# Edge sums by quarters of a group, a packed list in 96 partitions, and edge distances made on chip in a graph layer

## The chip, the cores and the metric

The kernel runs on one core of a Trainium2 chip. The metric is the device time of one execution in microseconds (us), as the median of several runs. TensorE is called PE (its weight loads PEld), VectorE DVE, ScalarE ACT, GpSimd POOL and SyncE SP. Line numbers such as L235 are those of the kernel before the change.

## The reference

`x` holds 6250 nodes of 64 features. 206250 edges are sorted by their target `dst`; each has a source `src` and 64 features of its own.

```python
h = jnp.maximum(_layernorm(x, axis=-1), 0.0)
msg = h[src] + edge_attr_64
agg = jax.ops.segment_sum(msg, dst, num_segments=6250)
y = jax.nn.relu(agg @ W1 + b1) @ W2 + b2
return x + y
```

## The kernel before

**Groups.** The edges are cut into G = 202 groups of 1024 (128 partitions by J = 8 edges). Of these, the first GA = 176 are the main groups and the last GP = 26 the part groups. The sum over `edge_attr_64` is made for all groups in the same way, by `sum_groups` (L227), two groups (GB = 2) at a time. As the edges are sorted, the targets of a group lie close together. DVE makes a mask `hot` (L229): for each edge a row of W = 40 numbers, one where the distance of the edge's target from the group's first target (`rel`) equals the column, else zero. PE multiplies, for each of the eight edges of a partition, the 128 edges' 64 features (as weights) by the mask (as moving operand, 40 columns) and sums in PSUM, `pa` (L235); even and odd edges go to the two halves of the partitions. The line appears twice in the profile's count for each product, since a product in f32 is two matmul instructions. One call later DVE adds `pa` to `agg` at the group's base (`add_sums`, L224); the base is a number in a register that DVE's sequencer reads (`read_bases`, four groups at a time in the main groups, L241).

`load` (L214) brings the features of two main groups by one DMA from SP's queue, three calls ahead; each partition receives its eight edges as one piece of 2 KB per group.

**The sum over h[src].** For the main groups it is made by counting. Every 84 windows of three nodes form one of NW = 22 batches, and a batch has 14 steps. At a step (`count`, L455) DVE makes the masks `hot_lo` and `hot_key` from the lists of sources (`keys`), PE multiplies them into a table of counts (L467) and ACT copies it out (L469). In the batch after, PE multiplies the counts by h, held as three bf16 pieces (`multiply`, L484 and L487), into `pv`, which DVE adds to `agg` (L499). For the part groups POOL gathers the rows of h instead and adds them to the edges' features by DMA (`fetch_h`, 208 gathers, L184).

**The lists.** The prologue makes them. `dst_g` is loaded as `dstn` (row q holds two groups of 1024 targets), `src` is transposed on PE into the same order (L270, copied out by ACT, L271), and DVE joins both into one word per edge (L277). The first QA = 89 rows are stored to DRAM as `packed` (L280, ACT's queue, 712 KB). For each of 1920 windows POOL then gathers 129 words from `packed` (`fetch_words`), from the place of the window's first edge. That place is found by gathers of rows of `dst_g` (`fetch_row`) and counts by DVE (`find`, L199 to L204). `unpack` (L322) splits the words on DVE (L326 to L331), transposes them on PE (L335, L336) and copies them to `keys` on ACT (L339).

`rel` is made by one DVE subtraction (L285) from `dst`, a load of all targets in the order of the groups (L111, 808 KB), less `row2`, the first targets of the groups, which a PE product (`pe`, L273) spreads to all partitions.

**The order.** All instructions of an engine run in the order in which the program writes them (`manual_schedule`). The step loop (L624) goes over 308 steps; before a step it runs what the table `before` (L591) holds for it: layer norm and lists up to step 11, `limits` at step 12, `seconds` at step 13 (the lists of windows with more edges than one gather takes) and the start of the part groups' gathers. From step 14 on, `features` (main groups) and `features_h` (part groups) are spread evenly over the steps. `limits` (L443) is one ACT pass over `rel`, which sums in `bad` what lies beyond the width of the mask, and one DVE comparison that does not read it. After the loop come the last batch's products and node blocks, and one DVE, PE and DVE sequence which decides whether the data fitted the shapes; if not, a slower loop computes all again, which the present data never enter.

**The nodes' network.** `mlp_hidden`, `mlp_product`, `mlp_add`, `mlp_store` (L534 to L555) run on blocks of up to 252 nodes as these become complete.

Of the kernel before, what the change touches and what calls it, by code (L numbers as in the profile page):

```python
# [18 lines left out]
P = 128  # L19
N = 6250  # L20
E = 206250
D = 64
# [8 lines left out]
J = 8  # L31
# [1 line left out]
GN = 256  # L33
GB = 2

W = 40
WR = 128
WR_BITS = 7
ACOLS = N + W + WR


GP = 26
# [37 lines left out]
def gnn_kernel(ctx: ExitStack, tc: tile.TileContext, x, src_t, dst_t, dst_g, edge, w1, b1, w2, b2, out):  # L80
# [47 lines left out]
    nc.scalar.activation(agg, zero.to_broadcast([P, ACOLS]), AF.Copy)  # L128

    HW = V * P  # L130
    iota_hw = small.tile([P, IC + 1], F32, name="iota_hw")
# [72 lines left out]
        nc.vector.tensor_scalar(first_i[:, i0:i0 + n], to, float(EA), None, op0=OP.min)  # L204


    rel = dst.bitcast(F32)
    base_i = consts.tile([1, G], I32, name="base_i")
    feats = {}
    bases = {}  # L210
# [3 lines left out]
    def load(g):  # L214
        feats[g] = work.tile([P, GB * J, D], F32, name="feat", bufs=3)
        nc.sync.dma_start(
            feats[g].rearrange("p (b j) d -> p b (j d)", j=J),
            edge[g * P * J:(g + GB) * P * J, :].rearrange("(b p j) d -> p b (j d)", p=P, j=J))

    def add_sums():  # L220
        for g, pa in to_add:
            for b in range(GB):
                to = agg[:, ds(bases.pop(g + b), W)]
                nc.vector.tensor_tensor(to, to, pa[:, b, :], op=OP.add)  # L224
        to_add.clear()

    def sum_groups(g, tiles):  # L227
        hot = work.tile([P, GB, J, W], F32, name="hot")
        nc.vector.tensor_tensor(hot, rel[:, g:g + GB, :].unsqueeze(3).to_broadcast([P, GB, J, W]),  # L229
                                iota[:, :W].unsqueeze(1).unsqueeze(1).to_broadcast([P, GB, J, W]), op=OP.is_equal)  # L230
        pa = ps.tile([P, GB, W], F32, tag="pa", name="pa")
        for b in range(GB):
            for j in range(J):
                k = j % 2 * D
                nc.tensor.matmul(pa[k:k + D, b, :], tiles[b][:, j, :], hot[:, b, j, :], start=(j < 2),  # L235
                                 stop=(j >= J - 2))
            done_at[g + b] = made[0] if g < GA else max(made)
        add_sums()
        to_add.append((g, pa))
# [24 lines left out]
    srcf = src.bitcast(F32)  # L264
    nc.scalar.activation(srcf, src, AF.Copy)
    srcv = srcf.rearrange("p (q h j) -> p q h j", h=2, j=J)
    for h in range(2):
        pt = ps.tile([P, J, P], F32, tag="pc", name="psrc")
        for j in range(J):
            nc.tensor.transpose(pt[:GA // 2, j, :], srcv[:, :, h, j], ident)  # L270
        nc.scalar.activation(srcl[:GA // 2, h].rearrange("q p j -> q j p"), pt[:GA // 2], AF.Copy)  # L271
# [10 lines left out]
    find(1, 2)  # L282
    for i in range(6, 9):
        fetch_row(i)
    nc.vector.tensor_tensor(rel, dst, row2.unsqueeze(2).to_broadcast([P, G, J]), op=OP.subtract)  # L285
# [144 lines left out]

    bad = small.tile([P, 2], F32, name="bad")
    edge_w = small.tile([P, 1], F32, name="edge_w")
    nc.gpsimd.memset(edge_w, 1.0 - W)
# [5 lines left out]
    evs = small.tile([P, NW * STEPS], F32, name="evs")  # L441

    def limits():  # L443
        nc.scalar.activation(late.tile([P, G * J], BF16, tag="part", name="over", bufs=2), rel.rearrange("p g j -> p (g j)"),
                             AF.Relu, bias=edge_w, accum_out=bad[:, 0:1])
        nc.vector.tensor_tensor(needed, row2[0:1, :], needed, op=OP.is_lt)


# [229 lines left out]
    sums = small.tile([1, 4], F32, name="sums")  # L678
    nc.vector.tensor_reduce(bad[:, 1:2], evs, AX.X, OP.add)
    pb = ps.tile([P, 2], F32, tag="pv", name="pb")  # L680
    nc.tensor.matmul(pb, ones, bad, start=True, stop=True)
    nc.vector.tensor_reduce(sums[:, 2:3], needed, AX.X, OP.max)
    nc.vector.tensor_scalar(sums[:, 0:1], pb[:1, 0:1], 0.0, None, op0=OP.is_gt)
    nc.vector.tensor_scalar(sums[:, 1:2], pb[:1, 1:2], float(EA), None, op0=OP.not_equal)
    odd_i = small.tile([1, 1], I32, name="odd_i")
    nc.vector.tensor_reduce(sums[:, 3:4], sums[:, :3], AX.X, OP.add)
    nc.vector.tensor_copy(odd_i, sums[:, 3:4])
    order.__exit__(None, None, None)


# [1 line left out]
    with tc.If(odd > 0):  # L692
        nc.vector.memset(agg, 0.0)

        dst2 = counts[0].rearrange("p h n -> p (h n)").bitcast(I32)[:, :2 * P * J].rearrange("p (h k) -> p h k", h=2)
        nc.sync.dma_start(dst2, dst_g)
        top = small.tile([P, 2], F32, name="top")
        nc.vector.tensor_reduce(top, dst2, AX.X, OP.max)
        diag2 = work.tile([P, P, 2], F32, tag="hot", name="diag2")
        nc.vector.tensor_tensor(diag2, ident.unsqueeze(2).to_broadcast([P, P, 2]),  # L700
                                top.unsqueeze(1).to_broadcast([P, P, 2]), op=OP.mult)
        pe2 = ps.tile([P, GN], F32, tag="pv", name="pe2")
        nc.tensor.matmul(pe2, ones, diag2.rearrange("p q h -> p (q h)"), start=True, stop=True)
        wide = small.tile([1, G], F32, name="wide")
        nc.vector.tensor_tensor(wide, pe2[0:1, :G], row2[0:1, :], op=OP.subtract)
        wide_i = small.tile([1, G], I32, name="wide_i")
        nc.vector.tensor_scalar(wide_i, wide, float(WR), None, op0=OP.add)
        nc.vector.tensor_scalar(wide_i, wide_i, WR_BITS, None, op0=OP.arith_shift_right)
        with tc.For_i(0, G, 1) as g:
            feat = work.tile([P, J, D], F32, tag="pfeat", bufs=4, name="feat2")  # L710
            hsrc = work.tile([P, J, D], F32, tag="pfeat", bufs=4, name="hsrc")
            nc.sync.dma_start(feat.rearrange("p j d -> p (j d)"),
                              edge.rearrange("(g p j) d -> g p (j d)", p=P, j=J)[ds(g, 1), :, :]
                              .rearrange("o p f -> (o p) f"))
            index = work.tile([P, J], I32, name="index", bufs=1)
            nc.sync.dma_start(index, src_t[:, ds(g * J, J)])
            left = work.tile([P, J], F32, name="left", bufs=1)
            nc.vector.tensor_copy(left, rel.rearrange("p g j -> p (g j)")[:, ds(g * J, J)])
# [58 lines left out]
```

## Time and profile before

| | |
|---|---|
| median of 3 runs | 604.29 us (603.38 to 604.59) |
| the profiled execution | 606.77 us, of which the profile's span is 605.1 us |
| mean granted PE clock | 0.905 |
| PE busy | 487.0 us (80% of the span) |
| DVE busy | 491.5 us (81%) |
| POOL busy | 401.7 us (66%) |
| ACT busy | 345.9 us (57%) |
| moved by DMA | 73.96 MB in 75905 packets |

The profile comes from one execution. "Busy" is the time in which an engine had an instruction at work. In lists of groups of instructions, a row has the line, the engine, the operation, the output and inputs with their shapes and the count; then the busy time of all and the mean of one in ns; then the idle time of the engine just before them and what ended it. In a timeline a row has the start, the length and the instruction, and in brackets the wait before it. In a list of waits the numbers are the total in us, the times and the longest. In the view by windows, the window and its length are followed by the busy time of PE, PEld, DVE, ACT and POOL with their instructions, the granted PE clock, the DMA share and GB/s. The queue q1 is SP's, q10 ACT's and q0 POOL's; after a queue's name stand packets, MB and the share of the time of 16 DMA engines.

### The profile page before, as it was taken

What the parts mean: (1) busy time and instruction counts of PE and PEld (TensorE: products, weight loads), DVE (VectorE), ACT (ScalarE), POOL (GpSimd) and SP (SyncE); (2) the same over time, 40 slices, a digit from 0 to 9 for tenths busy, and PEclk for the clock granted to TensorE, in tenths of its full rate; (3) what the DMA queues carried; (4) which work ended last, traced back from release to release, by engine and by line L of the source; (5) the groups of instructions that cost most, each with busy time, mean ns of one, the idle gap of its engine ahead of it and who ended that gap; (6) DMA issues with size and microseconds to landing.
All of it is one profiled execution on the core that took longest, in us unless ns stands there. A gap on an engine that the chain in (4) does not pass through costs nothing.

```text
span 605.1 us, 18376 instructions
## 1 busy us (share of the span) xinstructions
PE 487.0 (80%) x7529; PEld 410.5 (68%) x7530; DVE 491.5 (81%) x1120; ACT 345.9 (57%) x688; POOL 401.7 (66%) x258
## 2 busy tenths in 40 slices
PE   3000234799898998999999999999999999999993
PEld 2000123688786777788887887878888887888872
DVE  5501989699899988899998898898998899899821
ACT  7000467577575655666665665666666666666630
POOL 4503620588888888888888888888888888860000
PEclk9555555599999999999999999999999999999996
DMA  9701244156655654565655555465656565553000
GB/s 255 229 27 53 57 88 111 38 144 143 177 138 130 148 131 120 131 159 129 156 126 148 117 142 145 121 154 129 156 134 156 126 149 119 125 140 113 8 1 17
DMA packets 75905, 73.96 MB, mean 122 GB/s; under 512 B 40709, under 2 KB 48767, under 8 KB 75599
## 3 DMA queue, kind: packets, MB, share of 16 engines
q1 hardware_dynamic: 44398, 61.49, 32.6%
q0 software_dynamic: 31184, 9.80, 14.9%
q8 instruction: 61, 1.00, 0.7%
q10 hardware_dynamic: 234, 1.45, 0.6%
q14 instruction: 28, 0.23, 0.1%
HBM read 68.77 MB, written 3.93 MB: 120 GB/s over the span
## 4 chain that ended last, share of the span: by engine, by line
PE 62%; DVE 18%; issue 10%; ACT 3%; DMA 3%; DVEq 1%; POOL 0%; ACTq 0%
PE pc L467 19%; PE pv L484 15%; PE pa L235 12%; PE pv L487 10%; DVE hot_key L461 6%; DVE hot_lo L461 4%; DMA rows<-in_dst_g,row_i 2%; PE po L545 2%; DVE hot L229 2%; PE ph L538 2%; DVE agg L224 2%; ACT counts L469 1%; ACT keys L339 1%; DMA firsts_i<-in_dst_g 1%; PE pk L335 1%
## 5 line engine op out<-in xcount | busy, mean ns | idle before, releaser
L184 POOL DMA_INDIRECT pfeat<-table,src_p x208 | 365.2, 1756 | 63.4 <-issue 58.8
L469 ACT ACTIVATE counts<-pc 128x882 bf16<-128x882 f32 x308 | 279.8, 910 | 174.4 <-PE pc L467 157.5
L467 PE MATMUL pc<-hot_key,hot_lo 128*128 128x147 bf16 x1848 | 177.3, 234 | 34.8 <-DVE hot_key L461 27.8
L461 DVE TENSOR_TENSOR hot_key<-iota_key,keys 128x888 bf16<-128x888 bf16 x308 | 189.7, 616 | 0.0
L467 PEld LDWEIGHTS <-hot_lo 128*128 128x128 bf16 x1848 | 128.8, 100 | 66.2 <-DVE hot_key L461 39.1
L461 DVE TENSOR_TENSOR hot_lo<-iota_lo,keys 128x768 bf16<-128x768 bf16 x308 | 169.5, 550 | 1.1 <-issue 0.6
L484 PE MATMUL pv<-counts,h 128*128 128x252 bf16 x1078 | 147.5, 270 | 0.4 <-ACT counts L469 0.4
L484 PEld LDWEIGHTS <-h 128*128 128x128 bf16 x1078 | 98.8, 97 | 8.6 <-issue 0.6
L235 PEld LDWEIGHTS pa<-hot,feat 128*64 128x64 f32 x2816 | 92.7, 139 | 14.3 <-DVE hot L229 4.1
L235 PE MATMUL pa<-hot,feat 128*64 128x40 f32 x2816 | 100.2, 230 | 2.4 <-DVE hot L229 2.2
L229 DVE TENSOR_TENSOR hot<-dst,iota 128x640 f32<-128x640 f32 x101 | 82.5, 817 | 3.4 <-issue 3.4
L487 PE MATMUL pv<-counts,h 128*64 128x252 bf16 x1078 | 81.4, 276 | 0.0
L487 PEld LDWEIGHTS <-h 128*64 128x64 bf16 x1078 | 53.3, 109 | 14.8 <-issue 4.6
L469 ACT ACTIVATION_READ_ACCUMULATOR counts<-pc 128x1 f32 x308 | 59.4, 193 | 0.0
L335 PE MATMUL pk<-ident,klo 128*128 128x128 f32 (+1 forms) x16 | 7.0, 436 | 58.5 <-ACT klo L329 58.5
L224 DVE TENSOR_TENSOR agg<-agg,pa 128x40 f32 x202 | 38.9, 193 | 16.6 <-PE ph L538 5.7
L184 POOL DMA_INDIRECT words<-packed,first_i x15 | 15.6, 1042 | 44.6 <-DMA packed<-dstn 27.5
L335 PEld LDWEIGHTS pk<-ident,klo 128*128 128x128 f32 (+1 forms) x16 | 3.2, 200 | 61.3 <-ACT klo L329 61.3
L550 DVE TENSOR_TENSOR y<-xs,po 126x128 f32<-126x128 f32 (+2 forms) x25 | 7.2, 288 | 34.6 <-PE po L545 33.1
L329 ACT ACTIVATE klo<-klo 128x256 f32<-128x256 int32 (+2 forms) x9 | 3.5, 386 | 42.1 <-DVE klo L326 42.1
L184 POOL DMA_INDIRECT rows<-in_dst_g,row_i x15 | 16.6, 1104 | 11.6 <-DVE row_i L181 6.5
L326 DVE TENSOR_SCALAR klo<-words 128x256 int32<-128x256 int32 (+2 forms) x9 | 2.4, 270 | 25.6 <-DMA words<-packed,first_i 25.6
(125 smaller groups left out, 230.2 us busy)
## 6 DMA issues: line engine op xcount, KB each, us to landing
feat<-in_edge SPq DMA_DIRECT2D x88, 512.0 KB
pfeat<-in_edge SPq DMA_DIRECT2D x26, 256.0 KB
pfeat<-table,src_p POOLq DMA_INDIRECT x208
out_y<-y SPq DMA_DIRECT2D x23, 63.0 KB
dstn<-in_dst_g SPq DMA_DIRECT2D x1, 1024.0 KB
table<-xl SPq DMA_DIRECT2D x2, 512.0 KB
xs<-in_x SPq DMA_DIRECT2D x3, 315.0 KB
dst<-in_dst_t SPq DMA_DIRECT2D x1, 808.0 KB
```

The source lines that it names most:

```text
L184: nc.gpsimd.indirect_dma_start(out=rows, out_offset=None, in_=source, in_offset=bass.IndirectOffsetOnAxis(ap=index, axis=0), compute_op=op)
L224: nc.vector.tensor_tensor(to, to, pa[:, b, :], op=OP.add)
L229: nc.vector.tensor_tensor(hot, rel[:, g:g + GB, :].unsqueeze(3).to_broadcast([P, GB, J, W]), iota[:, :W].unsqueeze(1).unsqueeze(1).to_broa ...
L235: nc.tensor.matmul(pa[k:k + D, b, :], tiles[b][:, j, :], hot[:, b, j, :], start=(j < 2), stop=(j >= J - 2))
L335: nc.tensor.transpose(pk[:, 0, i, :p], klof[:p, i, :], ident[:p, :p])
L461: nc.vector.tensor_tensor(hot.rearrange("p t (m o) -> p t m o", o=2), iota_k.rearrange("p (m o) -> p m o", o=2).unsqueeze(1).to_broadcast( ...
L467: nc.tensor.matmul(pc[:, k, m * K:(m + 1) * K], hot_lo[:, j, :], hot_key[:, j, :K], start=True, stop=True)
L469: nc.scalar.activation(counts[b % 2][:, :, s * ST * V:(s + 1) * ST * V].rearrange("p h (k m) -> p h k m", k=2), pc[:, :, :ST // 2 * K].rea ...
L484: nc.tensor.matmul(pv, h3[:, h, :2 * D], counts[b % 2][:, h, :], start=(h == 0), stop=False)
L487: nc.tensor.matmul(pv[k:k + D, :], h3[:, h, 2 * D:], counts[b % 2][:, h, :], start=False, stop=(h >= HI - 2))
L538: nc.tensor.matmul(ph[:, :n], w1s, agg[:, start[b]:start[b + 1]], start=True, stop=True)
L545: nc.tensor.matmul(po[:pairs[b], k, :], outs[b][:, k:2 * pairs[b]:2], w2s, start=True, stop=True)
```

## The change

- **Quarters.** The edges of a main group are laid out in four quarters (JQ = 4) of 256 edges; in a quarter, a partition holds two edges (JP = 2). The mask of an edge is WQ = 18 columns wide, and the window of quarter q starts 8q - 5 nodes from the group's base; the matmul writes 18 of the 42 columns of `pa` (W = 8 x 3 + 18). A load of features has pieces of 512 B in place of 2 KB. The part groups keep whole groups, with W = 42.
- **Room below the base.** `agg` becomes a view of `sums`, which has OFF = 5 columns more in front.
- **The packed list.** QA = 96: `packed` and the join of words have 96 rows in place of 89.
- **Distances.** For the main groups, `rel` is no longer made from a load but from `dstn`: ACT copies it to f32 (into the place of `counts0`, not in use yet), PE transposes it in 16 pieces, and DVE subtracts the bases, of which ACT makes four copies shifted by quarters. Only the targets of the part groups are loaded (`dst_p`).
- **Bases.** The main groups' bases are read eight at a time.
- **The check.** `limits` has two ACT passes for each of `rel` and `rel_p` (too far and below zero), and a DVE reduction over their four sums, ahead of the DVE comparison.

```diff
-W = 40
+JQ = 4
+JP = J // JQ
+QS = 8
+WQ = 18
+OFF = 5
+W = QS * (JQ - 1) + WQ
...
-QA = GA // 2 + 1
+QA = 96
...
-    agg = consts.tile([P, ACOLS], F32, name="agg")
+    sums = consts.tile([P, OFF + ACOLS], F32, name="sums")
+    agg = sums[:, OFF:]
...
-    dst = consts.tile([P, G, J], I32, name="dst")
-    nc.sync.dma_start(dst, dst_t.rearrange("p (g j) -> p g j", j=J))
+    dst_p = consts.tile([P, GP, J], I32, name="dst_p")
+    nc.sync.dma_start(dst_p, dst_t.rearrange("p (g j) -> p g j", j=J)[:, GA:, :])
...
-            feats[g].rearrange("p (b j) d -> p b (j d)", j=J),
-            edge[g * P * J:(g + GB) * P * J, :].rearrange("(b p j) d -> p b (j d)", p=P, j=J))
+            feats[g].rearrange("p (b k) d -> p b (k d)", k=JP),
+            edge[g * P * J:(g + GB) * P * J, :].rearrange("(b p k) d -> p b (k d)", p=P, k=JP))
...
-        hot = work.tile([P, GB, J, W], F32, name="hot")
-        nc.vector.tensor_tensor(hot, rel[:, g:g + GB, :].unsqueeze(3).to_broadcast([P, GB, J, W]),
-                                iota[:, :W].unsqueeze(1).unsqueeze(1).to_broadcast([P, GB, J, W]), op=OP.is_equal)
         pa = ps.tile([P, GB, W], F32, tag="pa", name="pa")
+        if g < GA:
+            hot = work.tile([P, GB, J, WQ], F32, name="hot")
+            nc.vector.tensor_tensor(hot.rearrange("p b j w -> p (b j) w"),
+                                    rel[:, g:g + GB, :].rearrange("p b j -> p (b j)").unsqueeze(2)
+                                    .to_broadcast([P, GB * J, WQ]),
+                                    iota[:, :WQ].unsqueeze(1).to_broadcast([P, GB * J, WQ]), op=OP.is_equal)
...
+                if g < GA:
+                    o = QS * (j // JP)
+                    to = pa[k:k + D, b, o:o + WQ]
...
-        if g % (2 * GB) == 0:
-            read_bases(g, 2 * GB)
+        if g % (4 * GB) == 0:
+            read_bases(g, 4 * GB)
...
+    dstf = counts[0].rearrange("p h n -> p (h n)").bitcast(F32)[:, :2 * P * J].rearrange("p (h k) -> p h k", h=2)
+    nc.scalar.activation(dstf[:GA // 2], dstn[:GA // 2], AF.Copy)
...
-    nc.vector.tensor_tensor(rel, dst, row2.unsqueeze(2).to_broadcast([P, G, J]), op=OP.subtract)
+    rowq = pr.tile([P, JQ, GA], F32, name="rowq")
+    for q in range(JQ):
+        nc.scalar.activation(rowq[:, q, :], pe[:, :GA], AF.Copy, bias=float(QS * q - OFF))
+    dstv = dstf.rearrange("q h (j p k) -> q h j p k", j=JQ, k=JP)
+    for h in range(2):
+        pt = ps.tile([P, JQ, JP, P], F32, tag="pc", name="pdst")
+        for q in range(JQ):
+            for k in range(JP):
+                nc.tensor.transpose(pt[:, q, k, :GA // 2], dstv[:GA // 2, h, q, :, k], ident[:GA // 2, :GA // 2])
+        nc.vector.tensor_tensor(
+            rel.rearrange("p (g h) (q k) -> p q k g h", h=2, k=JP)[:, :, :, :, h], pt[:, :, :, :GA // 2],
+            rowq.rearrange("p q (g h) -> p q g h", h=2)[:, :, :, h].unsqueeze(2).to_broadcast([P, JQ, JP, GA // 2]),
+            op=OP.subtract)
...
     def limits():
-        nc.scalar.activation(late.tile([P, G * J], BF16, tag="part", name="over", bufs=2), rel.rearrange("p g j -> p (g j)"),
-                             AF.Relu, bias=edge_w, accum_out=bad[:, 0:1])
+        over = late.tile([P, GA * J], BF16, tag="part", name="over", bufs=2)
+        for k, a in enumerate((rel, rel_p)):
+            a = a.rearrange("p g j -> p (g j)")
+            nc.scalar.activation(over[:, :a.shape[1]], a, AF.Relu, bias=edge_w[:, k:k + 1],
+                                 accum_out=bad[:, 2 * k:2 * k + 1])
+            nc.scalar.activation(over[:, :a.shape[1]], a, AF.Relu, scale=-1.0,
+                                 accum_out=bad[:, 2 * k + 1:2 * k + 2])
+        nc.vector.tensor_reduce(bad[:, 4:5], bad[:, :4], AX.X, OP.add)
         nc.vector.tensor_tensor(needed, row2[0:1, :], needed, op=OP.is_lt)
```

The rest of the diff follows from these: a second place for the part groups' mask (`hotp`), six columns of `bad` in place of two, the tile of the last decision renamed `found`, and the targets loaded anew in the slower loop.

More of the change, by code (lines that the diff above doesn't have):

```diff
@@ L72 @@
 NR = GN * P * J // L1 // P
-QA = GA // 2 + 1
+QA = 96
+assert QA > GA // 2
 DUMP = N + 2
@@ L127, in gnn_kernel @@
     nc.scalar.activation(root, zero, AF.Sqrt)
-    nc.scalar.activation(agg, zero.to_broadcast([P, ACOLS]), AF.Copy)
+    nc.scalar.activation(sums, zero.to_broadcast([P, OFF + ACOLS]), AF.Copy)
     HW = V * P
@@ L204, in find @@
         nc.vector.tensor_scalar(first_i[:, i0:i0 + n], to, float(EA), None, op0=OP.min)
-    rel = dst.bitcast(F32)
+    rel = consts.tile([P, GA, J], F32, name="rel")
+    rel_p = dst_p.bitcast(F32)
     base_i = consts.tile([1, G], I32, name="base_i")
@@ L222, in add_sums @@
             for b in range(GB):
-                to = agg[:, ds(bases.pop(g + b), W)]
+                to = sums[:, ds(bases.pop(g + b), W)]
                 nc.vector.tensor_tensor(to, to, pa[:, b, :], op=OP.add)
@@ L227, in sum_groups @@
     def sum_groups(g, tiles):
-        hot = work.tile([P, GB, J, W], F32, name="hot")
-        nc.vector.tensor_tensor(hot, rel[:, g:g + GB, :].unsqueeze(3).to_broadcast([P, GB, J, W]),
-                                iota[:, :W].unsqueeze(1).unsqueeze(1).to_broadcast([P, GB, J, W]), op=OP.is_equal)
         pa = ps.tile([P, GB, W], F32, tag="pa", name="pa")
+        if g < GA:
[4 more added lines that the diff above has]
+                                    iota[:, :WQ].unsqueeze(1).to_broadcast([P, GB * J, WQ]), op=OP.is_equal)
+        else:
+            hot = work.tile([P, GB, J, W], F32, name="hotp", bufs=1)
+            nc.vector.tensor_tensor(hot, rel_p[:, g - GA:g - GA + GB, :].unsqueeze(3).to_broadcast([P, GB, J, W]),
+                                    iota[:, :W].unsqueeze(1).unsqueeze(1).to_broadcast([P, GB, J, W]),
+                                    op=OP.is_equal)
         for b in range(GB):
@@ L234, in sum_groups @@
                 k = j % 2 * D
-                nc.tensor.matmul(pa[k:k + D, b, :], tiles[b][:, j, :], hot[:, b, j, :], start=(j < 2),
-                                 stop=(j >= J - 2))
+                if g < GA:
+                    o = QS * (j // JP)
+                    to = pa[k:k + D, b, o:o + WQ]
+                else:
+                    to = pa[k:k + D, b, :]
+                nc.tensor.matmul(to, tiles[b][:, j, :], hot[:, b, j, :], start=(j < 2), stop=(j >= J - 2),
+                                 skip_group_check=(g < GA))
             done_at[g + b] = made[0] if g < GA else max(made)
@@ L676, in gnn_kernel @@
         assert done_at[g] <= 0 or done_at[g] <= 31 * (g - GA) + NEED_P, (g, done_at[g], 31 * (g - GA) + NEED_P)
-    sums = small.tile([1, 4], F32, name="sums")
-    nc.vector.tensor_reduce(bad[:, 1:2], evs, AX.X, OP.add)
+    found = small.tile([1, 4], F32, name="found")
+    nc.vector.tensor_reduce(bad[:, 5:6], evs, AX.X, OP.add)
     pb = ps.tile([P, 2], F32, tag="pv", name="pb")
[L681 to L684, printed above, removed]
+    nc.tensor.matmul(pb, ones, bad[:, 4:6], start=True, stop=True)
+    nc.vector.tensor_reduce(found[:, 2:3], needed, AX.X, OP.max)
+    nc.vector.tensor_scalar(found[:, 0:1], pb[:1, 0:1], 0.0, None, op0=OP.is_gt)
+    nc.vector.tensor_scalar(found[:, 1:2], pb[:1, 1:2], float(EA), None, op0=OP.not_equal)
     odd_i = small.tile([1, 1], I32, name="odd_i")
-    nc.vector.tensor_reduce(sums[:, 3:4], sums[:, :3], AX.X, OP.add)
-    nc.vector.tensor_copy(odd_i, sums[:, 3:4])
+    nc.vector.tensor_reduce(found[:, 3:4], found[:, :3], AX.X, OP.add)
+    nc.vector.tensor_copy(odd_i, found[:, 3:4])
     order.__exit__(None, None, None)
```

13 lines of the change are left out of this document (9 added, 4 removed).

## The prediction

> **What bounds the kernel now.** I read the profile's summary first, then the timeline of the first 60 us, then the waits and the busy time of the long middle part, and last the groups of instructions that the diff touches.
>
> ```profile
> PE 487.0 (80%) x7529; PEld 410.5 (68%) x7530; DVE 491.5 (81%) x1120; ACT 345.9 (57%) x688; POOL 401.7 (66%) x258
> ...
> PE   3000234799898998999999999999999999999993
> ...
> DVE  5501989699899988899998898898998899899821
> ...
> DMA  9701244156655654565655555465656565553000
> ```
>
> One slice is 15 us. There are three parts: slices 2 and 3, in which PE, DVE and the transfers are all nearly idle; a climb to about 118 us; and a long part in which PE is at nine tenths and DVE close behind. The change touches all three, so each is priced by itself. The idle part, in the timeline (start, length, instruction, wait before it):
>
> ```profile
> 16.74 0.49 ACTq L280 DMA_DIRECT2D packed<-dstn  x1
> ...
> 24.76 0.96 POOL L184 DMA_INDIRECT rows<-in_dst_g,row_i  x1 [0.16 <-DVE first_i L204]
> ...
> 31.57 0.17 DVE L204 TENSOR_SCALAR first_i<-first 128x4 int32<-128x4 f32 x1
> ...
> 53.25 0.95 POOL L184 DMA_INDIRECT words<-packed,first_i  x1 [27.53 <-DMA packed<-dstn]
> ...
> 57.34 0.29 DVE L326 TENSOR_SCALAR klo<-words 128x256 int32<-128x256 int32 x1 [25.61 <-DMA words<-packed,first_i]
> ```
>
> The store of the packed list, issued at 16.74, is not there until 53.25, when the first gather from it may start; DVE stands still for 25.61 us, and all else stands behind it. Why it takes so long is in the DMA view of 26 to 50 us (first two lines) against that of 2 to 9 us (last line), both for the queue of ACT:
>
> ```profile
> DMA packets 162, 0.76 MB, mean 32 GB/s; under 512 B 30, under 2 KB 38, under 8 KB 92
> ...
> q10 hardware_dynamic: 70, 0.57, 5.6%
> ...
> q10 hardware_dynamic: 134, 0.66, 26.1%
> ```
>
> In 24 us only 0.57 MB of the list move, in 70 packets of a whole row (8 KB), and the share is 5.6% where one of 16 engines would be 6.25%. The list of 89 rows goes through one engine. The load of src, 128 rows on the same queue, moved 0.66 MB inside 7 us, on more than four engines' worth of time. The long part, 118 to 580 us, in busy time and in waits:
>
> ```profile
> 118.00:580.00 462.00, 443.08 (x7149) 375.71 (x7147) 418.60 (x952) 296.41 (x609) 360.03 (x206) 1.00 0.54 133
> ```
> ```profile
> PEld L467 <- DVE hot_key L461: 22.0, 46, 1.6
> ...
> PE pc L467 <- DVE hot_key L461: 12.4, 28, 1.5
> ...
> PEld pa L235 <- DVE hot L229: 5.7, 9, 1.0
> ...
> PE pa L235 <- DVE hot L229: 3.4, 8, 0.7
> ```
>
> PE is busy 443.08 of 462 us at full clock: it bounds this part. What it loses to DVE is 12.4 + 3.4 = 15.8 us by its matmuls' rows and 22.0 + 5.7 = 27.7 us by its weight loads' rows (which include time in which the array still worked). I take 22 us. That is the most that a faster DVE can give here.
>
> **The change, part by part.** *The packed list in 96 partitions.* Ninety-six rows, like 128, divide into sixteen equal shares of whole rows; 89 do not divide at all. The trace has no row of 96, so the bounds are the two rows above: like 89 rows, which gains nothing and costs 2 us more (7 more rows of 8 KB at 0.57 MB in 24 us), or like 128 rows. I take the second. "DMA: Bandwidth & Descriptors" of the Trainium skill, section "Why a DMA increments its semaphore by 16 and not by 1", says that a transfer runs on the largest number of engines, up to 16, that divides its slowest dimension, and names 96 partitions as 16 engines and a prime as one; by that the store has all engines, and the one-engine row for 89 agrees.
>
> What is late next? The store is issued at 16.74 and the engines also carry the three first feature loads; with everything spread I put its end before 26 us. POOL issues its last gather before the list until 24.76 + 0.96 = 25.7, and from the first list gather to the first use of its words is 57.34 - 53.25 = 4.1 us, so words are there at about 30.1. DVE meanwhile works until 31.57 + 0.17 = 31.7, and that becomes the end that counts: 57.34 - 31.7 = 25.6 us are saved. If the store is late by 4 us the gain is 22; if the row gathers, freed of the crowded engine, let DVE finish earlier, 27.5.
>
> *Distances by transposes on chip.* Sixteen transposes, a copy of the list to float, four copies of the bases and two subtractions replace one load and one subtraction:
>
> ```profile
> L270 PE MATMUL psrc<-ident,src 128*88 128x128 f32 x16 | 3.4, 404 | 0.9 <-ACT src L265 0.9
> ...
> L271 ACT ACTIVATE srcl<-psrc 88x1024 int32<-88x1024 f32 x2 | 3.9, 2051 | 2.1 <-PE psrc L270 2.1
> ...
> L285 DVE TENSOR_TENSOR dst<-dst,row 128x1616 f32<-128x1616 int32 x1 | 1.8, 1841 | 0.0
> ```
>
> The sixteen transposes of src take PE 3.4 us, and the new sixteen will take about as much, at a time when PE has nothing else. The float copy, 2048 wide, goes at about 2 us (two of L271's 1024-wide copies take 3.9, from PSUM) into the 2.1 us in which ACT waits for the transposes at L271. The subtractions are 1408 + 208 elements, as many as the 1616 of L285; with two more starts 2.0 to 2.6 us against 1.84. All of this ends before DVE's next wait for row gathers, and the packed store stays where it is. I cost it at nothing; if the cover is gone, 0.8 us. The load that goes (704 of 808 KB) only clears the queue earlier.
>
> *The check in limits.* One ACT pass with one wait-free DVE instruction behind it becomes four passes, and a DVE reduction that waits for them. This is the part where the change adds a wait. From the timeline at step 12:
>
> ```profile
> 104.29 0.35 DVE L446 TENSOR_TENSOR needed<-row,needed 1x202 f32<-1x202 f32 x1
> ...
> 105.04 0.60 DVE L461 TENSOR_TENSOR hot_key<-iota_key,keys 128x888 bf16<-128x888 bf16 x1
> 107.74 0.17 DVE L404 TENSOR_SCALAR fl<-behind 128x15 f32<-128x15 f32 x1 [2.09 <-ACT behind L342]
> ...
> 108.94 1.63 ACT L444 ACTIVATE over<-dst,edge_w 128x1616 bf16<-128x1616 f32 x1
> ...
> 112.74 0.54 DVE L461 TENSOR_TENSOR hot_lo<-iota_lo,keys 128x768 bf16<-128x768 bf16 x1
> ```
>
> DVE reaches this place at 104.29, ACT only at 108.94. ACT's four passes are 2 x (1408 + 208) elements, by L444's row 2 x 1.63 = 3.3 us and a little for two more starts, so they end near 112.5. DVE then stands from 104.3 to 112.5. Queued behind it are the masks of step 12 (0.54 + 0.60 us) and the search for second lists (L404 on), which now begins at 112.5 + 0.1 + 0.35 + 1.14 = 114.1 instead of 107.74: 6.3 us later. It ends in the masks of step 13 (112.74), on which PE, and by the second list also POOL's long row of gathers, wait; the PE-bound part starts 6.3 us later. Bounds: 2 us if only the added ACT time counts, 8 if PE and ACT queue up worse.
>
> *Masks 18 wide.*
>
> ```profile
> L229 DVE TENSOR_TENSOR hot<-dst,iota 128x640 f32<-128x640 f32 x101 | 82.5, 817 | 3.4 <-issue 3.4
> ...
> L392 DVE TENSOR_TENSOR part<-xl,h 128x1024 f32<-128x1024 f32 x2 | 2.4, 1219 | 0.0
> ```
>
> From 640 to 1024 elements DVE takes 402 ns more, 1.05 ns each. The 88 masks of the main groups shrink from 640 to 288: 817 - 352 x 1.05 = 448 ns, 88 x 0.37 = 32.5 us of DVE time; the 13 others grow to 672, 0.4 us in all. DVE's 418.6 us of 462 become 386, but DVE doesn't bound: only PE's 22 us of waiting can be won. Part of that waiting has other reasons (DVE itself waits for PE before y and agg), so I take two thirds, 15 us, bounds 4 and 21.
>
> On PE the moving operand of 2816 matmuls goes from 40 to 18 columns. Whether that shortens anything is read from weight loads of different width (timelines near 224, 304 and 301 us):
>
> ```profile
> 223.78 0.46 PEld L545 LDWEIGHTS po<-w2s,hid 128*102 128x102 f32 x4 [0.20 <-issue]
> ...
> 303.57 0.54 PEld L545 LDWEIGHTS po<-w2s,hid 128*126 128x126 f32 x4
> ...
> 301.55 1.01 PEld L235 LDWEIGHTS pa<-hot,feat 128*64 128x64 f32 x32 [0.21 <-issue]
> 301.56 1.13 PE L235 MATMUL pa<-hot,feat 128*64 128x40 f32 x32
> ```
>
> The same four products with 102 instead of 126 weight columns and equal moving columns take 0.08 us less, 0.02 each, 0.83 ns a column: the weights set the pace there. At that rate 64 columns are 53 ns, and the 32 loads of L235, two halves of the array at a time, 16 x 53 = 0.85 of their 1.01 us. So the weights bound L235 too, and 18 columns give nothing but the last matmul's shorter run: 22 columns, some 0.02 us a call, -1 us in all (0 to -2). [...]
>
> *Feature loads in pieces of 512 B, bases by eight.* A load of 512 KB goes from 256 pieces of 2 KB to 1024 of 512 B. From the DMA views of 300 to 500 us (two lines) and 62 to 94 us (the last, nearly all pieces of 256 B):
>
> ```profile
> q1 hardware_dynamic: 13815, 24.19, 36.9%
> q0 software_dynamic: 14350, 3.27, 18.9%
> ...
> q1 hardware_dynamic: 6303, 1.60, 25.1%
> ```
>
> 0.369 x 16 x 200 us / 13815 = 85 ns for 1751 B; 0.251 x 16 x 32 / 6303 = 20 ns for 254 B. On the line between them 512 B cost 31 ns, 2 KB 98. Four for one adds 26 ns to each of 88 x 256 pieces: 37 us on each engine over 450 us, 54% busy becomes some 62%. Loads are issued three groups ahead, so this hides: nothing. Reading bases by eight halves the readings; the mask's own 3.4 us of "issue" bounds what that can give (0 taken, -2 to +1).
>
> **The rivals.** (1) *Still one engine*: 96 rows behave as 89 did. For it: no row shows 96. Then +2 + 6.3 - 15 - 1 = -8, about 597. (2) *Moving columns pace L235*: 1.13 us a call falls by 22/40 of its 0.85 us stream, 0.3 to 0.5 us, 88 calls, 26 to 41 us less on PE; with DVE at 386 us it would show, some 24 us below my forecast, 545. Against it are the two L545 rows. (3) *POOL becomes the bound*:
>
> ```profile
> L184 POOL DMA_INDIRECT pfeat<-table,src_p x208 | 365.2, 1756 | 63.4 <-issue 58.8 <-PE pc L467 1.2 <-DMA pfeat<-table,src_p 1.2
> ...
> 538.84 1.96 POOL L184 DMA_INDIRECT pfeat<-table,src_p  x1 [0.30 <-issue]
> ...
> 562.75 1.13 PE L235 MATMUL pa<-hot,pfeat 128*64 128x40 f32 x32
> ```
>
> The 208 gathers run without a break, 365 + 63 = 428 us, whatever PE does; the last ends at 540.8 and is used at 562.75, 22 us of room. My 16 us leave 6. If the finer pieces slow the gathers by 5%, 21 us, PE waits 15: 584. It decides from 1.4% on. (4) *The other side: a piece costs by the packet, not by the byte.* If 512 B took the 85 ns of the mean piece, 88 loads would need 88 x 1024 x 85 ns / 16 = 479 us of every engine; gathers (0.149 x 605 = 90, from the queue's share on the page) and the rest of q1 (0.326 x 605 - 88 x 256 x 85 ns / 16 = 77) make 646: the transfers would bound, about 645, slower. The page's queue rows are these:
>
> ```profile
> q1 hardware_dynamic: 44398, 61.49, 32.6%
> q0 software_dynamic: 31184, 9.80, 14.9%
> ```
>
> Loads run from 14 to about 585 us, so it decides from some 72 ns a piece; 20 ns for 254 B speaks against it.
>
> **How the numbers follow.** -25.6 + 6.3 - 15 - 1 = -35.3 us on the profiled execution, 606.77 us (span 605.1): 571.5. That execution is 2.5 us above the median of the runs, 604.29, so 569.0 for the median. All ends at once would be 604.29 - 50.5 = 554 and 604.29 - 16 = 588; not all meet, so 555 to 585, which takes in most of rival 3. Chances: forecast 0.74, rival 1 0.06, rival 2 0.07, rival 3 0.10, rival 4 0.03. All but rival 4 are faster by far more than 0.2% (1.2 us, about what a measurement of this kernel can tell from no change): faster 0.96, the same 0.01, slower 0.03.
>
> **What would show it.** Right: DVE's first wait for words shrinks from 25.6 us to under 2 and the empty slices go; a DVE wait of some 8 us for ACT at the new reduction, step 12; the mask near 0.45 us; 32 matmuls of L235 still near 1.0 us; PE's waits for hot_key cut by more than half. Wrong: packed still landing 30 us after its issue; L235 well under 0.9 us a call; PE waiting for gathers in the last 100 us; DMA at nine tenths throughout.

## The result, and the profile after

The kernel after takes 575.32 us (median; 575.13 to 575.45), the kernel before, run beside it, 603.92 us: a ratio of 0.9526, interval 0.9509 to 0.9542, or 28.6 us less. The profiled execution of after took 575.13 us, its span 573.4 us. The forecast was 569.0 us in a range of 555 to 585. On the page of after, engines first, then the slices (14.3 us each):

```profile
PE 489.4 (85%) x7545; PEld 415.8 (73%) x7546; DVE 462.7 (81%) x1123; ACT 352.7 (62%) x699; POOL 399.0 (70%) x259
...
PE   3132428998999999999999999999999999999993
...
DVE  5898937897999788988878989779888879798801
...
DMA  8822501666576555766556665665657565654000
```

The two empty slices are gone, and PE is at nine tenths from slice 7 on instead of slice 8 (counted from 0). The prologue and the place of the check, in the timeline of after:

```profile
16.77 0.34 ACTq L306 DMA_DIRECT2D packed<-dstn  x1
...
24.68 0.94 POOL L193 DMA_INDIRECT words<-packed,first_i  x1 [0.40 <-DMA packed<-dstn]
...
27.96 0.17 DVE L213 TENSOR_SCALAR first_i<-first 128x4 int32<-128x4 f32 x1
...
28.55 0.29 DVE L366 TENSOR_SCALAR klo<-words 128x256 int32<-128x256 int32 x1 [0.42 <-DMA words<-packed,first_i]
...
84.11 0.16 DVE L492 TENSOR_REDUCE bad<-bad 128x1 f32<-128x4 f32 x1 [8.79 <-ACT over L490]
...
85.46 0.16 DVE L444 TENSOR_SCALAR fl<-behind 128x15 f32<-128x15 f32 x1
...
89.58 0.53 DVE L508 TENSOR_TENSOR hot_lo<-iota_lo,keys 128x768 bf16<-128x768 bf16 x1
```

The store is there 7.9 us after its issue, where it took 36.5 us. DVE's wait for the first words is 0.42 us instead of 25.61, and it starts on them at 28.55 instead of 57.34, 28.8 us earlier. At the new reduction (L492) DVE stands 8.79 us for ACT, and the masks of step 13 come at 89.58 instead of 112.74: only 23.2 us are left.

The long part is best compared between the same two steps. The counts of step 20 and of the last step are copied out at 125.9 and 579.4 us in the kernel before, at 104.1 and 547.5 us in after. Busy time between them (window, length, then PE, PEld, DVE, ACT, POOL, the clock, DMA share, GB/s), first before:

```profile
125.90:579.40 453.50, 435.20 (x7045) 368.91 (x7045) 410.84 (x933) 290.40 (x597) 353.03 (x204) 1.00 0.54 134
```

and after:

```profile
104.10:547.50 443.40, 432.73 (x7045) 370.29 (x7045) 380.49 (x931) 292.14 (x597) 350.10 (x204) 1.00 0.60 136
```

With the same 7045 matmuls the part is 10.1 us shorter. PE's busy time fell by 2.5 us, and its idle time (length less busy) from 18.3 to 10.7 us. DVE has 30 us less to do. The sum over the execution: -28.8 at the first words, +5.6 to step 13, then from step 13 to step 20 125.9 - 112.74 = 13.16 us before against 104.1 - 89.58 = 14.52 us after, +1.4, then -10.1: 31.9 less, and the spans differ by 31.7.

### The profile page after: what moved, and what is told of

Its sections match the earlier page's. It is cut to its first block, busy times and chain, and to the rows that moved or that the text cites. A ratio compares the mean times of both kernels' runs of the same rounds, so it can differ in the third digit from the quotient of the medians.

```text
span 573.4 us, 18398 instructions
## 1 busy us (share of the span) xinstructions
PE 489.4 (85%) x7545; PEld 415.8 (73%) x7546; DVE 462.7 (81%) x1123; ACT 352.7 (62%) x699; POOL 399.0 (70%) x259
## 4 chain that ended last, share of the span: by engine, by line
PE 60%; DVE 8%; issue 2%; DVEq 1%; DMA 1%; ACT 1%; ACTq 0%
PE pc L514 18%; PE pv L531 15%; PE pa L259 12%; PE pv L534 10%; DVE hot_key L508 3%; PE po L592 2%; PE ph L585 2%; DVE hot_lo L508 2%; DVE sums L234 1%; DMA pfeat<-in_edge 1%; DVE hot L241 0%; DVE sums L556 0%; DVE y L597 0%; DVEq L266 0%; ACT counts L516 0%
## 5 line engine op out<-in xcount | busy, mean ns | idle before, releaser
L514 PEld LDWEIGHTS <-hot_lo 128*128 128x128 bf16 x1848 | 130.5, 101 | 64.5 <-DVE hot_key L508 46.2
L531 PE MATMUL pv<-counts,h 128*128 128x252 bf16 x1078 | 149.4, 272 | 0.4 <-ACT counts L516 0.4
L259 PEld LDWEIGHTS pa<-hot,feat 128*64 128x64 f32 x2816 | 92.7, 139 | 11.8 <-issue 4.0
L259 PE MATMUL pa<-hot,feat 128*64 128x18 f32 x2816 | 98.6, 212 | 0.3 <-DVE hot L241 0.3
L234 DVE TENSOR_TENSOR sums<-sums,pa 128x42 f32 x202 | 39.6, 196 | 30.2 <-PE ph L585 16.3
L241 DVE TENSOR_TENSOR hot<-rel,iota 128x288 f32<-128x288 f32 x88 | 39.6, 450 | 0.4 <-issue 0.4
L587 ACT ACTIVATE hid<-ph,b1s 128x252 f32<-128x252 f32 (+2 forms) x25 | 11.7, 470 | 15.7 <-PE ph L585 15.4
L193 POOL DMA_INDIRECT words<-packed,second_i x1 | 0.9, 864 | 25.6 <-DVE second_b L467 25.6
```

The source lines that it names most:

```text
L193: nc.gpsimd.indirect_dma_start(out=rows, out_offset=None, in_=source, in_offset=bass.IndirectOffsetOnAxis(ap=index, axis=0), compute_op=op)
L241: nc.vector.tensor_tensor(hot.rearrange("p b j w -> p (b j) w"), rel[:, g:g + GB, :].rearrange("p b j -> p (b j)").unsqueeze(2) .to_broadc ...
L259: nc.tensor.matmul(to, tiles[b][:, j, :], hot[:, b, j, :], start=(j < 2), stop=(j >= J - 2), skip_group_check=(g < GA))
L514: nc.tensor.matmul(pc[:, k, m * K:(m + 1) * K], hot_lo[:, j, :], hot_key[:, j, :K], start=True, stop=True)
L531: nc.tensor.matmul(pv, h3[:, h, :2 * D], counts[b % 2][:, h, :], start=(h == 0), stop=False)
L587: nc.scalar.activation(outs[b][:, :n], ph[:, :n], AF.Relu, bias=b1s)
```

## The experiments

The theory after the result was: one number, the 96 rows, carries the gain; the check gives some 6 us back; the narrow masks win 10 us through PE's waits for DVE, and the moving columns nothing. Times are compared by the difference to the kernel before on the same chip, which had medians of 605.93, 603.59 and 606.49 us in the three groups of runs.

**Only the packed list.** The kernel before with one line changed.

```diff
-QA = GA // 2 + 1
+QA = 96
```

> The kernel before with one number changed: the packed list has 96 rows in place of 89. Theory A (the number of rows decides how many DMA engines carry the store): the store lands some 8 us after its issue, the first words are used near 29 us as in the kernel after (28.55) instead of 57.34, and the time falls by 28 to 29 us, to about 575.5, all that the whole change gave, since what the rest of it gains in the long part (10 us) it loses again at its check and around it (7 us). Rival B (the earlier list comes from the smaller loads and the transposes of the prologue): the store still lands 30 us late or more and the time stays above 595.

Measured: 578.50 us, 27.4 less (ratio 0.9541, 0.9526 to 0.9557). Its timeline:

```profile
16.71 0.34 ACTq L280 DMA_DIRECT2D packed<-dstn  x1
...
26.06 0.95 POOL L184 DMA_INDIRECT words<-packed,first_i  x1 [0.30 <-issue]
...
29.60 0.17 DVE L204 TENSOR_SCALAR first_i<-first 128x4 int32<-128x4 f32 x1
29.95 0.30 DVE L326 TENSOR_SCALAR klo<-words 128x256 int32<-128x256 int32 x1 [0.18 <-issue]
```

Theory A, and a little under the 28 to 29 us that it expected: POOL no longer waits for the store at all, and DVE starts on the words as soon as its own search (L204) is done, which ends 2 us earlier than before (31.57). The unchanged kernel after, run again beside other runs, was 29.2 us below the kernel before (ratio 0.952, 0.9494 to 0.9545):

> The kernel after, unchanged, as the measure for the runs beside it on this chip. Both theories: some 28 us less than the kernel before, 4.5 to 5%.

So all else in the change is worth about 2 us together; the two differences come from two chips, and the runs of the list alone spread over 3 us.

**Ninety rows.** After, with `QA = 90`.

> The kernel after with the packed list in 90 rows in place of 96. Theory A (the store runs on as many engines, up to 16, as divide the rows evenly; 90 has 15): like 96 rows within 2 us, words used near 29 us. Rival B (only multiples of 16 or 32 rows are spread, or few engines are used otherwise): the store lands later, by up to 29 us.

Measured: 577.14 us, 29.3 less than before (two runs; ratio 0.9517, 0.9498 to 0.9536), as with 96 rows. From its timeline, and the queue of the store from 17 to 25 us:

```profile
16.78 0.72 ACTq L306 DMA_DIRECT2D packed<-dstn  x1
24.61 0.94 POOL L193 DMA_INDIRECT words<-packed,first_i  x1 [0.31 <-issue]
```
```profile
q10 hardware_dynamic: 105, 0.74, 22.2%
```

So it is not the multiple of 16 or 32 that matters. The store's packets took 0.222 x 16 x 8 = 28 us of one engine's time and were all there within 7.8 us of the issue, so at least four engines worked. 89, 90 and 96 rows together fit the rule that the prediction took from "DMA: Bandwidth & Descriptors" of the Trainium skill (section "Why a DMA increments its semaphore by 16 and not by 1"): 90 divides by 15, 89 by nothing up to 16. That exactly 15 engines work is not seen here, and other rules by which 89 alone is bad would fit as well.

**The reduction at the end.** After, with DVE's reduction over the four sums moved from `limits` to the last decision.

```diff
     def limits():
...
-        nc.vector.tensor_reduce(bad[:, 4:5], bad[:, :4], AX.X, OP.add)
         nc.vector.tensor_tensor(needed, row2[0:1, :], needed, op=OP.is_lt)
...
+    nc.vector.tensor_reduce(bad[:, 4:5], bad[:, :4], AX.X, OP.add)
     nc.vector.tensor_reduce(bad[:, 5:6], evs, AX.X, OP.add)
```

> The kernel after, with the DVE reduction over the four sums of limits moved from step 12 to the end of the kernel, beside the other last reduction; the four ACT passes stay. Theory A (the wait of DVE for ACT at this reduction, 8.79 us in the profile after, sets the start of the PE-bound part): DVE goes on at once, the search for second lists starts some 5 to 6 us earlier, and the time falls by 4 to 6 us from 575.3, to 569.5 to 571. Rival B (the ACT passes themselves delay, not the wait): 573 to 575.

Measured: 570.50 us, 35.4 less than before (ratio 0.9424, 0.9393 to 0.9455); after is 28.6 to 29.2 less, so by this run the wait was worth 6 to 7 us; the runs of this kernel spread over 3.7 us. DVE's timeline shows it go on:

```profile
75.62 0.35 DVE L492 TENSOR_TENSOR needed<-row,needed 1x202 f32<-1x202 f32 x1
...
79.07 0.17 DVE L444 TENSOR_SCALAR fl<-behind 128x15 f32<-128x15 f32 x1 [2.10 <-ACT behind L382]
...
84.06 0.54 DVE L507 TENSOR_TENSOR hot_lo<-iota_lo,keys 128x768 bf16<-128x768 bf16 x1
```

The search for second lists (L444) begins 6.4 us earlier than in after (85.46), the masks of step 13 5.5 us. Moving the ACT passes too, to step 24:

> The kernel with the late reduction, and all of limits (four ACT passes and the DVE comparison) at step 24, in the long part. Theory A (with the reduction gone, the passes at step 12 still delay ACT's copy of counts and with it the search for second lists): another 1 to 3 us less than with the late reduction alone. Rival B (the DVE wait was all): within 1 us of it.

Measured: 569.95 us, 33.6 less than before (ratio 0.9438, 0.9413 to 0.9463). It brought nothing more that these runs can tell, so nothing speaks for theory A: by the medians it is 0.6 us faster than the late reduction alone, by the differences to the kernel before 1.8 us slower. Rival B fits, but its 1 us is finer than the spread. Against after beside it on the same chip (574.42) this kernel is 4.5 us faster, so the wait was worth 4.5 to 7 us.

**Wide masks, and wide products.** After, with the main groups' masks 40 columns wide on DVE, of which PE moves 18; and a second kernel in which PE moves all 40.

```diff
-            hot = work.tile([P, GB, J, WQ], F32, name="hot")
+            hot = work.tile([P, GB, J, 40], F32, name="hot")
...
-                                    iota[:, :WQ].unsqueeze(1).to_broadcast([P, GB * J, WQ]), op=OP.is_equal)
+                                    iota[:, :40].unsqueeze(1).to_broadcast([P, GB * J, 40]), op=OP.is_equal)
...
-                nc.tensor.matmul(to, tiles[b][:, j, :], hot[:, b, j, :], start=(j < 2), stop=(j >= J - 2),
+                nc.tensor.matmul(to, tiles[b][:, j, :], hot[:, b, j, :to.shape[-1]], start=(j < 2), stop=(j >= J - 2),
```

> The kernel after, with the masks of the main groups made 40 columns wide again on DVE while PE still moves 18 of them. Theory A (the long part got shorter by DVE's shorter masks, through PE's waits for hot_key): the mask costs 0.82 us again, DVE is as full as before, and the time grows by 6 to 10 us, to 581 to 585. Rival B (the long part got shorter on PE, by 18 moving columns): within 2 us of 575.3.

> As the run with wide masks, and PE also moves 40 columns of them into a pa tile of 64 columns, of which DVE adds 42. Theory A (weight loads pace these matmuls): a call's 32 matmuls keep their 1.0 us, only each run to the next different weights grows by 0.02 us, 1 to 2 us in all over the run with wide masks alone. Rival B (the moving columns pace them): 26 us or more over it.

Measured: 582.67 us (23.3 less than before; ratio 0.9623, 0.9596 to 0.965) and 582.78 us (23.1 less; 0.9618, 0.9601 to 0.9634). The wide masks cost 5 to 6 us of the gain by these differences. In the trace the long part between the same two steps is 450.7 us, 7.3 us more than in after, as theory A expected, and PE stands idle for 17.1 us of it instead of 10.7:

```profile
105.30:556.00 450.70, 433.57 (x7043) 368.77 (x7043) 410.63 (x932) 290.01 (x597) 349.05 (x204) 1.00 0.59 134
```

PE's 22 additional columns on top of them cost 0.1 us by the medians. The runs of each of the two kernels spread over 1.5 to 3 us, so the 1 to 2 us of theory A are not excluded; the 26 us of rival B are. The groups of instructions with 18 moving columns and wide masks, and with 40:

```profile
L259 PE MATMUL pa<-hot,feat 128*64 128x18 f32 x2816 | 98.6, 212 | 1.7 <-DVE hot L241 1.4 <-issue 0.2
L259 PEld LDWEIGHTS pa<-hot,feat 128*64 128x64 f32 x2816 | 92.7, 139 | 13.7 <-issue 4.3 <-DVE hot L241 3.5 <-DVE sums L234 2.7
L241 DVE TENSOR_TENSOR hot<-rel,iota 128x640 f32<-128x640 f32 x88 | 71.8, 815 | 0.4 <-issue 0.4
```
```profile
L259 PE MATMUL pa<-hot,feat 128*64 128x40 f32 x2816 | 100.2, 230 | 1.7 <-DVE hot L241 1.4 <-issue 0.2
L259 PEld LDWEIGHTS pa<-hot,feat 128*64 128x64 f32 x2816 | 92.7, 139 | 13.7 <-issue 3.8 <-DVE hot L241 3.5 <-DVE hot_lo L508 2.5
```

The weight loads take 92.7 us in both, and the matmuls' busy time moves by 1.6 us for 2816 x 22 columns. The weights pace these products.

**Pieces of 2 KB.** After, with the loads laid out as before the change.

```diff
-            feats[g].rearrange("p (b k) d -> p b (k d)", k=JP),
-            edge[g * P * J:(g + GB) * P * J, :].rearrange("(b p k) d -> p b (k d)", p=P, k=JP))
+            feats[g].rearrange("p (b j) d -> p b (j d)", j=J),
+            edge[g * P * J:(g + GB) * P * J, :].rearrange("(b p j) d -> p b (j d)", p=P, j=J))
```

> The kernel after with the feature loads of the main groups in pieces of 2 KB as before; the edges then lie in the old order while masks and windows are those of quarters, so the sums take the wrong edges, with the same instructions. Theory A (the pieces of 512 B hide behind the three loads in flight): DMA share of the long part some 5 points lower, time within 1 us of the kernel after. Rival B (the finer pieces slow the gathers or the loads): 2 us or more faster.

Measured: 574.13 us against 574.42 us of after beside it (29.5 and 29.2 less than before): no difference. The queue of the loads, 277 to 477 us, with pieces of 2 KB:

```profile
q1 hardware_dynamic: 13937, 24.42, 38.7%
```

and in after with pieces of 512 B:

```profile
q1 hardware_dynamic: 43988, 24.39, 42.2%
```

Three times the packets cost this queue 3.5 points of the engines' time.

**Where PE's waits come from.** The narrow masks gave less than forecast, so the question was what keeps PE waiting in after. DVE's and PE's waits there, 104.1 to 547.5 us (total, times, longest):

```profile
DVE y L597 <- PE po L592: 23.6, 22, 2.4
DVE sums L234 <- PE ph L585: 16.3, 14, 2.8
DVE sums L234 <- PE pa L259: 9.9, 8, 2.8
PE pc L514 <- DVE hot_key L508: 9.1, 21, 1.3
```

and one place where it happens, in the timeline of after:

```profile
363.49 0.57 PE L592 MATMUL po<-w2s,hid 128*126 128x64 f32 x4
...
364.10 0.29 DVE L597 TENSOR_TENSOR y<-xs,po 126x128 f32<-126x128 f32 x1 [1.21 <-PE po L592]
364.30 0.55 DVE L508 TENSOR_TENSOR hot_lo<-iota_lo,keys 128x768 bf16<-128x768 bf16 x1
364.77 0.61 DVE L508 TENSOR_TENSOR hot_key<-iota_key,keys 128x888 bf16<-128x888 bf16 x1
...
365.44 0.56 PE L514 MATMUL pc<-hot_key,hot_lo 128*128 128x147 bf16 x6 [0.45 <-DVE hot_key L508]
```

DVE had run ahead of PE and stood 1.21 us for a node block's product, `po`. Only then came the masks of the next step, and PE in its turn waited for them. Two kernels move the addition `y` (and its store) one step away from `po`: one on top of the late reduction, one as the only edit of the kernel before.

```diff
-        for k, f in ((0, mlp_hidden), (2, mlp_product), (3, mlp_add), (5, mlp_store)):
+        for k, f in ((0, mlp_hidden), (2, mlp_product), (4, mlp_add), (6, mlp_store)):
```

> The kernel with the late reduction, and each node block's last addition (DVE, y from po) one step later than before, the store with it. Theory A (PE's remaining 12 to 13 us of waits in the long part come after DVE itself stood still for PE, at y for po and at the sums for ph): with a step more between po and y, DVE stands less (23.6 us at y falls below 8), PE's waits for hot_key fall with it, and the time falls by 3 to 6 us against the kernel with the late reduction alone, which was 6.8 us below the kernel after. Rival B (PE's waits come from DVE's own work, whatever it waits for): no more than 1 us.

> The kernel before with one edit: each node block's last DVE addition, and its store, one step later. Theory A (DVE standing at y for po is a cause of PE's waits in the kernel before as well, 17.8 us of DVE waits at y there, but DVE's wide masks leave it full, 90% busy): 3 to 6 us less, fewer than the 8 us that the same edit gave with narrow masks. Rival B (with wide masks DVE bounds what PE waits for, and where DVE stands does not matter): no more than 1 us.

Measured: 560.61 us, 43.0 less than before (ratio 0.9283, 0.9264 to 0.9303), with narrow masks and the late reduction, some 8 us below the late reduction alone; and 598.12 us, 8.4 less (0.9861, 0.9844 to 0.9877), for the edit alone in the kernel before. The long part between the same two steps, with narrow masks, and the waits at y and for hot_key in it:

```profile
98.60:536.00 437.40, 430.86 (x7045) 371.05 (x7044) 382.12 (x931) 291.59 (x597) 345.21 (x204) 1.00 0.61 138
```
```profile
DVE y L596 <- PE po L591: 3.1, 10, 0.7
...
PE pc L513 <- DVE hot_key L507: 5.8, 10, 1.3
```

and the kernel before with the edit alone:

```profile
126.50:571.80 445.30, 434.02 (x7045) 370.86 (x7044) 409.70 (x932) 289.03 (x597) 348.51 (x204) 1.00 0.55 136
```

PE's idle time is 18.3 us before, 10.7 with narrow masks, 11.3 with the later addition alone, 6.5 with both. So DVE's stand at `y` is a cause of PE's waits in both kernels, and it cost more than the 3 to 6 us expected; that the edit would gain less with wide masks did not come out. In the kernel before, with DVE 90% busy, moving one addition took about as much of PE's idle time away as 30 us less of DVE's work. The other part of theory A, the stand at the sums, is not shown: with narrow masks and the later addition DVE waits there even longer than in after (18.9 us for `ph`, 15.4 for `pa`). The store moves with the addition in both kernels; it was not moved by itself.

**The node blocks after the sums.** On top of this, the blocks' steps were written behind the edge sums of a step, so that DVE's addition to `sums` no longer stands for `ph`.

```diff
-        for f in mlps.pop(n, []):
-            f()
         if n >= STEPS:
...
+        for f in mlps.pop(n, []):
+            f()
```

> The kernel with the late reduction and the later addition, and the node blocks' steps written after the edge sums of the same step instead of ahead of them, so that DVE's addition to sums no longer comes behind the block's first product (ph), which reads sums. Theory A (DVE's wait at sums for ph, 18.9 us there, is what is left of PE's waits): it falls below 5 us and the time by 2 to 5 us. Rival B (PE is as full as it gets, 433 of 440 us busy): within 1 us.

A miss for both: 565.87 us, 40.6 less than before (ratio 0.9333, 0.9317 to 0.935), 2.4 us less gain than without it. DVE's waits, 100 to 540 us:

```profile
DVE sums L234 <- PE pc L513: 10.0, 7, 3.1
DVE y L596 <- PE po L591: 9.8, 10, 1.6
DVE sums L234 <- PE ph L584: 9.4, 12, 1.9
```

The wait for `ph` halved, to 9.4 us and not below 5, and others took its place, at `y` and at `sums` for `pc`. The kernel with the late reduction and the later addition is the fastest of all, 0.9283 of before.

## Why the prediction was right, and where it was off

**The packed list: right mechanism, under-sized.** The forecast was 25.6 us with a bound of 27.5; the first words are used 28.8 us earlier in after and 27.4 with the list alone. The prediction let DVE's own search end at 31.7 as before. It ends at 29.77 with the list alone and at 28.13 in after, as DVE waits less for the row gathers: 6.6 us from 14 to 34 us before, 4.6 with the list alone, 1.3 in after. That the store's crowded engine had held these gathers up, as the prediction's bound of 27.5 supposed, fits the list alone but is not shown; what the further step in after comes from, no run separates.

**Distances by transposes: right.** The two subtractions are slower than estimated, 1329 ns each and 342 ns for the rest, 3.0 us against 2.0 to 2.6, and hidden all the same: after uses its first words no later than the kernel with the list alone.

**The check: right.** Forecast +6.3 us, 5.6 to step 13 in the trace, 4.5 to 7 by the runs without the wait. The long wait stands where it was put, 8.79 us.

**The masks: the size of the mask right, what it is worth wrong.** The forecast of 448 ns for a mask met 450:

```profile
L241 DVE TENSOR_TENSOR hot<-rel,iota 128x288 f32<-128x288 f32 x88 | 39.6, 450 | 0.4 <-issue 0.4
```

The step that failed is "I take two thirds, 15 us" of "PE's 22 us of waiting". The long part became 10.1 us shorter, of which idle time of PE is 7.6; the masks alone are 7.3 of it, by the kernel with wide masks. PE's waits for `hot_key` were to fall by more than half; by its matmuls' rows they fell from 12.4 to 9.1 us (those for `hot` from 3.4 to 0.3). The prediction had named the reason, that DVE itself waits for PE before `y` and `agg`, and gave it too little weight. In the long part DVE worked 30 us less and stood 20 us longer (443.40 - 380.49 = 62.9 us against 453.50 - 410.84 = 42.7). It stood longer at `y` and, more so, at the sums; the waits of the kernel before, 125.9 to 579.4 us, against 23.6, 16.3 and 9.9 in after:

```profile
DVE y L550 <- PE po L545: 17.8, 17, 1.6
...
DVE agg L224 <- PE ph L538: 5.7, 9, 1.3
...
DVE agg L224 <- PE pa L235: 4.3, 4, 1.7
```

Two thirds of the time that DVE saved was spent standing. How long a stand is does not tell what it costs: taking away the one at `y`, which had grown the least in proportion, gave some 8 us, and halving the one for `ph` gave nothing.

**Moving columns: right.** 1.6 us of busy time for the 22 columns, and 0.1 us of time, by the two wide kernels; the second rival (26 to 41 us) falls. **Pieces of 512 B: right**, and with them the fourth rival falls; the DMA share rose from 0.54 to 0.60, forecast 0.62. The third rival, POOL as the bound, did not come up: the gathers still run without a break, PE's waits name none of them, and the last one ends at 516.1 us in after and is used at 530.9, with 15 us of room. The first rival falls with the first experiment.

**Not foreseen.** From step 13 to step 20 after needs 1.4 us more, the granted clock there being 0.65 against 0.78 in the kernel before:

```profile
89.58:104.10 14.52, 13.30 (x146) 11.21 (x147) 12.91 (x33) 7.41 (x17) 12.99 (x6) 0.65 0.26 53
```
```profile
112.74:125.90 13.16, 11.42 (x146) 9.90 (x147) 12.94 (x31) 7.40 (x17) 11.94 (x5) 0.78 0.24 53
```

PE got its full clock later after the start of the dense work: six products of `pc` take 0.92 us at half clock and 0.55 at full clock, and the change comes some 5 us after the first of them in the kernel before and some 9 in after. The stand at the check does not decide it. The same kernel in another execution needs 13.5 us at a clock of 0.70; the list alone, without the stand, 13.8 at 0.68; the kernel with wide products, with the stand, 13.1 at 0.79. The stretch varies from execution to execution, and its length goes with the clock.

**The step from the profile to the median.** The profiled execution of before lies 2.9 us above its median, and the prediction took 2.5 us off the execution of after, which lies level with its own. Against the profiled executions the forecast of -35.3 met -31.6; against the medians -28.6.

**How the errors add up.** By the trace the list gave 3.2 us more than forecast and the check cost 0.7 less; the masks and columns gave 5.9 less, and 1.4 were not foreseen: -35.3 becomes -31.9. That the list's error took back half of the masks' is luck.

## What to carry to other kernels

Read the bandwidth of a single transfer in the stage that waits for it: 0.57 MB in 24 us and a share of one sixteenth pointed to nearly the whole gain of this change, and one line brought 27.4 of its 29 us. Before time saved on an engine is counted, look where that engine itself stands for the bound one: here DVE had 30 us less to do and stood 20 us longer, and moving one addition away from its wait gave about as much. A wait that is added ahead of a chain makes the engine stand for as long as the awaited engine is behind at that place, here 8.8 us for a reduction of 0.16 us, of which 4.5 to 7 us came through to the end; where its result is not needed until then, it can go to the end.

## What the runs showed of the hardware

- The same store of a list, from 89 rows, took 36.5 us until its reader could start, from 90 or 96 rows (in after) no more than 7.9.
- Products of 64 f32 weight columns cost the same with 18 and with 40 moving columns: weight loads 92.7 us in both.
- The record of the granted clock can lack a stretch at half clock. The page of the kernel before with the later addition alone has full clock from the start:

```profile
PEclk9999999999999999999999999999999999999995
```

But in its timeline six products of `pc` take 0.95 us in the climb, as in the kernel before, where the record has half clock, and 0.55 us later:

```profile
104.20 0.95 PE L467 MATMUL pc<-hot_key,hot_lo 128*128 128x147 bf16 x6
...
121.59 0.55 PE L467 MATMUL pc<-hot_key,hot_lo 128*128 128x147 bf16 x6
```

So two executions of the kernel before with spans of 603.7 and 603.9 us at mean granted clocks of 0.993 and 0.906 do not show that the half clock in the climb costs nothing.
